# A transformer layer with eight experts: the order of the last pair of tiles, the loading of the first expert matrix, and the order of the last output block

## The chip, the cores and the metric

The kernel runs on one core of a Trainium2 chip. The metric is the device time of one execution in microseconds; lower is better. The core has five engines with queues of their own: TensorE (PE, matrix products; its weight loads are shown as PEld), VectorE (DVE), ScalarE (ACT), GpSimd (POOL) and SyncE (SP), which issues most of the DMAs here. Each engine works through its instructions in the order in which they stand in its queue; semaphores join the queues.

## The reference, cut to what matters

Everything is float32. There are 32 batches of 32 tokens with 512 features (1024 tokens) and a context of 257 rows per batch.

```python
x = x + cross_attention(layernorm(x), ctx)        # one head, 257 keys
x = x + self_attention(layernorm(x))              # 16 heads of 32, rotary, 32 tokens a batch
x = x + experts(layernorm(x))

# experts(xf): 8 experts, the best 2 for each token
scores = sigmoid(xf @ gate_w.T + balance_bias)
top, idx = top_k(scores, 2)
top = top / (top.sum(-1) + 1e-6)
comb[token, idx] = top
h = silu(einsum("td,ehd->teh", xf, w1))           # 512 -> 1024
out = einsum("te,ted->td", comb, einsum("teh,edh->ted", h, w2))
```

## The kernel before, in words

The 1024 tokens are eight tiles of 128 rows, kept in `x_sb`. Two tiles are a pair, `p` from 0 to 3. After the cross-attention comes the self-attention pair by pair, and interleaved with it the routing of the pair before.

The steps of a pair, each a small function in the source:

- `norm`, `turn`: layer norm and transposes through TensorE (tile `yT`).
- `project(p, j, half)`: a quarter of the queries or keys, 16 TensorE instructions (`pp`). A product of 32-bit numbers shows as two instructions.
- `scores(p, i)`: 128 small 32x32 products (`pqs`), then maximum and subtraction on DVE (`smx`, `sex`), exponential on ACT. The PSUM tile has one buffer (`psq`), which `attend` uses too.
- `shares(p, i)`: sum, reciprocal, product and transpose on DVE (`ssm`, `aT`).
- `values(p, tiles)`: the value products (`ppv`) and a copy on ACT.
- `attend(p, i)`: 128 small products (`pos`), then a bias on DVE (`oT`).
- `finish(p, i)`: output projection (`ppo`), addition to `x_sb` on DVE, and a DMA of the row block to the output through SP.
- `norm2(p, i)`: row statistics and the normalized row `fy`, with its token number, for the experts.
- `gate_turn(p, i)`: four transposes of `x_sb` (`fpt`) and a copy on ACT (`fyT`). `gate_logits(p, i)`: eight TensorE instructions with eight columns each (`pg`), then `lg` on DVE. `gate` is both.
- `pick(p)`: the two best experts and their weights, some twenty small DVE instructions with a little ACT and POOL; the running count `cc` is made on POOL, the marks `mk` on DVE.
- `places(p)`: four small products (`pr`) give each token its place in its expert's list, DVE makes it a row number (`pi`), and POOL scatters the rows with four indirect DMAs to the lists `xs_d` in memory.

The loop over `p` = 0, 1, 2 runs the attention of pair `p`, projects pair `p + 1` and routes pair `p - 1`. The last pair (p = 3) is written out behind it. There `order()` ranks the experts by the rows that they have from the first three pairs: four small products (`pn`), seven small DVE instructions, then SP reads the expert numbers into registers and issues the loads: the first expert's `w1` (2 MB in two DMAs), its first 256 rows (`xse`, which must wait until the scatters of the first three pairs have landed), its `w2`, and, after seven more register loads, the second expert's `w1`. `early_turn`, `early_hidden(0)` to `early_hidden(7)` and `early_out` compute these 256 rows of the first expert (`xpe`, `phe`, `poe`) while the last pair is still being routed.

Behind the attention come the remaining rows of the first expert and then the other seven in turn (`turn_rows`, `hidden`, `output`). The list of expert number r in the ranking is computed for `WIDTH[r]` rows: whole blocks of 128 and a part. In `output` a whole block is 16 products of 512 columns (`fpo`), a part is 64 or more small ones (`fpq`); each result is scaled on DVE (`fob`) and added to the output rows by an indirect DMA from POOL that accumulates (`add_rows`, line 194). Rows of a list that hold no token go to spare rows behind the 1024 real ones. Two additions to the output are ordered by a semaphore unless the source declares them independent. The last expert has 160 rows: one block and a part of 32.

The order on each engine is made when the program is built, from the order of the source, by a planner that may put a ready instruction ahead of one that it expects to wait. Buffers of a tile pool are freed by the last reader; the four PSUM buffers `ps` serve most products.

Of the kernel before, what the change touches and what calls it, by code (L numbers as in the profile page):

```python
# [9 lines left out]
F32 = mybir.dt.float32  # L10
# [7 lines left out]
P = 128  # L18
# [4 lines left out]
D = 512  # L23
DC = 384
KD = D // P
# [3 lines left out]
NTT = 8  # L29
NE = 8  # L30
FF = 1024
# [4 lines left out]
WIDTH = (384, 352, 288, 288, 288, 224, 192, 160)  # L36
CAP = max(WIDTH)
NB = CAP // P
EARLY = 2
Q = 32  # L40
YI, YC, YW = D, D + 8, D + 16
# [10 lines left out]
def tile_perceiver_layer(  # L52
# [138 lines left out]
        nc.vector.bn_aggr(mv, st)  # L191

    def add_rows(dst, ob, place, n):
        nc.gpsimd.indirect_dma_start(  # L194
            out=dst,
            out_offset=bass.IndirectOffsetOnAxis(ap=place, axis=0),
            in_=ob,
            in_offset=None,
            bounds_check=n * (NTT * P + P) - 1,
            oob_is_err=True,  # L200
            compute_op=ALU.add,
        )
# [22 lines left out]
    with ExitStack() as attn:  # L225
# [606 lines left out]
        with ExitStack() as sa:  # L832
# [265 lines left out]
            def order():  # L1098

                full = [P, NE, NE]  # L1100
                c = counts(cums[-1], "cnt0")
                key = keep.tile([P, NE], F32, name="key")
                nc.vector.scalar_tensor_tensor(
                    key, c, float(NE), down, op0=ALU.mult, op1=ALU.add
                )
                above = keep.tile(full, F32, name="above")
                nc.vector.tensor_tensor(
                    above,
                    key.unsqueeze(1).to_broadcast(full),
                    key.unsqueeze(2).to_broadcast(full),  # L1110
                    ALU.is_gt,
                )
                rank = keep.tile([P, NE], F32, name="rank")
                nc.vector.tensor_reduce(rank, above, AX.X, ALU.add)

                hot = keep.tile(full, F32, name="hot")
                nc.vector.tensor_tensor(
                    hot,
                    rank.unsqueeze(1).to_broadcast(full),
                    iof.unsqueeze(2).to_broadcast(full),  # L1120
                    ALU.is_equal,
                )
                he = keep.tile(full, F32, name="he")
                nc.vector.tensor_tensor(
                    he, hot, iof.unsqueeze(1).to_broadcast(full), ALU.mult
                )
                eid = keep.tile([P, NE], F32, name="eid")
                nc.vector.tensor_reduce(eid, he, AX.X, ALU.add)
                eidi = keep.tile([P, NE], I32, name="eidi")
                nc.vector.tensor_copy(eidi, eid)  # L1130
                tail["hot"] = hot

                def expert(r):
                    return nc.values_load(
                        eidi[0:1, r : r + 1], engines=[mybir.EngineType.SP],
                        min_val=0, max_val=NE - 1,
                    )


                e = expert(0)  # L1140
                tail["w1"] = {0: expert_w1(e)}
                xs = wk.tile([P, 2, YW], F32, tag="y", name="xse")
                nc.sync.dma_start(
                    xs, xs_d[bass.ds(e * LIST, 2 * P), :].rearrange("(c p) w -> p c w", p=P)
                )
                tail["w2"] = {0: expert_w2(e)}
                tail["e"] = [e] + [expert(r) for r in range(1, NE)]
                tail["w1"][1] = expert_w1(tail["e"][1])
                he0 = keep.tile([P, NE], F32, name="he0")
                nc.vector.tensor_tensor(he0, hot[:, 0, :], c, ALU.mult)  # L1150
                had = keep.tile([P, 1], F32, name="had")
                nc.vector.reduce_sum(had, he0, axis=AX.X)
                mask = keep.tile([P, EARLY], I32, name="mask")
                nc.vector.tensor_scalar(mask, slot[:, 0, 0:EARLY], had, 0.0, ALU.is_lt, ALU.add)
                pl = keep.tile([P, EARLY], I32, name="pl")
                nc.vector.tensor_copy(pl, spare.to_broadcast([P, EARLY]))
                tail["had"] = had
                tail["early"] = {"xs": xs, "mask": mask, "pl": pl}
# [56 lines left out]
            turn(1)  # L1215
            for p in range(NP - 1):
                scores(p, 0)
                project(p + 1, 0, 0)
                shares(p, 0)
                scores(p, 1)  # L1220
                if p:
                    gate(p - 1, 0)
                    gate(p - 1, 1)
                    pick(p - 1)
                project(p + 1, 0, 1)
                shares(p, 1)
                rotate(p + 1, 0)
                attend(p, 0)
                project(p + 1, 1, 0)
                step(norm, p + 2)  # L1230
                attend(p, 1)
                if p:
                    places(p - 1)
                project(p + 1, 1, 1)
                rotate(p + 1, 1)
                finish(p, 0)
                norm2(p, 0)
                finish(p, 1)
                norm2(p, 1)
                if p < NP - 2:  # L1240
                    values(p + 1)
                    step(turn, p + 2)
# [3 lines left out]
            scores(p, 0)  # L1246
            gate_turn(p - 1, 0)
            gate_turn(p - 1, 1)
            scores(p, 1)
            gate_logits(p - 1, 0)  # L1250
            gate_logits(p - 1, 1)
            pick(p - 1)
            values(p, (0,))
            shares(p, 0)
            places(p - 1)
            attend(p, 0)
            values(p, (1,))
            order()
            shares(p, 1)
            finish(p, 0)  # L1260
            norm2(p, 0)
            attend(p, 1)
            gate(p, 0)
            finish(p, 1)
            norm2(p, 1)
            early_turn()
            gate_turn(p, 1)
            early_hidden(0)
            gate_logits(p, 1)
            pick(p)  # L1270
            early_hidden(1)
            early_hidden(2)
            places(p)
            cnt = counts(cums[-1], "cnt")
# [22 lines left out]
    )  # L1297
    idx = keep.tile(full, I32, name="idx")
    nc.gpsimd.iota(
        idx, pattern=[[0, NE], [0, LIST // P]], base=NTT * P, channel_multiplier=1  # L1300
    )
    def parts_of(n):
        return [(c, min(P, n - c * P)) for c in range((n + P - 1) // P)]
# [38 lines left out]
    def short_part(hT, w2, q, place, sh):  # L1342
# [10 lines left out]
                )  # L1353
        ob = fw.tile([P, D], F32, tag="fob", bufs=3, name="fob")
        nc.vector.tensor_scalar_mul(ob[:, 0:w], po[:, 0:w], sh)  # L1355
        add_rows(out.rearrange("r (n w) -> (r n) w", n=n), ob[:, 0:w], place, n)

    def turn_rows(r, xs, n, taken, idx):

# [58 lines left out]
                nc.tensor.transpose(pt[:, k, :], t["hs"][:, ts(h * KD + k, P)], ident)  # L1418
            evac(h, t["hT"][:, h * KD : (h + 1) * KD, 0:P], pt)

    def output(t, w2):

        hT, share, idx = t["hT"], t["share"], t["idx"]
        parts = parts_of(t["n"])
        for c, m in parts:
            if m < P:
                for r0, q in tails_of(m):
                    short_part(
                        hT[:, :, c * P + r0 : c * P + r0 + q], w2, q, *t["spread"].pop(0)
                    )  # L1430
        for c, m in parts:
            if m < P:
                continue
# [5 lines left out]
                )  # L1439
            ob = fw.tile([P, D], F32, tag="fob", bufs=3, name="fob")  # L1440
            nc.vector.tensor_scalar_mul(ob, po, share[:, c : c + 1])  # L1441
            add_rows(out, ob, idx[:, c : c + 1], 1)


    rows_of = {
# [8 lines left out]
    for r in range(1, NE):  # L1454
# [8 lines left out]
        if r == 1:  # L1463
# [1 line left out]
            w1s[2] = expert_w1(eids[2])  # L1465
            rows_of[2] = load_rows(eids[2], 0, WIDTH[2])
            w2s[2] = expert_w2(eids[2])
        output(t, w2s.pop(r))


    over = keep.tile([P, NE + 1], F32, name="over")
# [131 lines left out]
```

## Time and profile before

| | |
|---|---|
| median of 3 runs | 566.55 us (565.16 to 568.67) |
| the profiled execution | 567.44 us |
| its span, first to last instruction | 565.6 us |
| granted TensorE clock, mean | 0.972 |
| PE / DVE / ACT / POOL busy | 93% / 43% / 22% / 19% |
| last pair, from its first scores to `early_out` | 258.6 to 311.6 us |
| remaining rows and other experts | to 554.2 us |

In the profile a line like `L979` is a line of the kernel, `out<-in` names tiles, and `x8` counts instructions. Times are microseconds from the start of the span. Where a line ends with a bracket, it gives the idle time of the engine before it and who ended it. A granted clock of 0.50 means that TensorE got every second pulse.

### The profile page before, as it was taken

To read this page: it belongs to the slowest core of one execution; us is meant where nothing else is said; L and a number is where in the kernel's file an instruction comes from. 1 tells how busy PE (TensorE), PEld (TensorE's weight loads), DVE (VectorE), ACT (ScalarE), POOL (GpSimd) and SP (SyncE) were. 2 spreads that over 40 slices of the span, in tenths; PEclk is the share of its full clock that TensorE was granted. 3 is DMA by queue.
4 is the path that set the end of the run, shared out by engine and by line. 5 is a ranking of instruction groups with operands and counts; after the bars stand their busy time and mean duration, and the time that the engine had idled before them with its cause. 6 is when DMAs were issued, how large, how long until landed. Compare 5 with 4: busy or idle time off the path is not lost.

```text
span 565.6 us, 11308 instructions
## 1 busy us (share of the span) xinstructions
PE 527.2 (93%) x4718; PEld 342.4 (61%) x4718; DVE 243.2 (43%) x706; ACT 123.9 (22%) x274; POOL 105.5 (19%) x185
## 2 busy tenths in 40 slices
PE   6999998999999999998979999999999999999991
PEld 3555554566584875876548456547657475768570
DVE  6564668646667755668534032203122121223120
ACT  3444444322313312212022021002011010102010
POOL 2323445120001012022302110122120202111211
PEclk9899999999999999798989999999999999999997
DMA  7999968999920002012296332647653554756521
GB/s 271 389 376 400 307 248 281 363 393 386 385 84 38 3 21 94 4 41 78 79 366 232 91 92 77 235 135 215 172 167 111 132 192 155 215 159 197 160 27 22
DMA packets 43135, 104.56 MB, mean 185 GB/s; under 512 B 4001, under 2 KB 7233, under 8 KB 42050
## 3 DMA queue, kind: packets, MB, share of 16 engines
q1 hardware_dynamic: 38482, 94.96, 46.9%
q0 software_dynamic: 4592, 8.78, 7.7%
q8 instruction: 39, 0.64, 0.5%
q14 instruction: 22, 0.18, 0.1%
HBM read 75.55 MB, written 28.18 MB: 183 GB/s over the span
## 4 chain that ended last, share of the span: by engine, by line
PE 67%; DMA 2%; DVE 2%; issue 1%; ACT 1%; POOL 0%; POOLq 0%; SPq 0%; ACTq 0%
PE ph L1383 18%; PE fpo L1436 15%; PE pp L387 8%; PE ppv L857 5%; PE fpq L1350 4%; PE phe L1187 3%; PE poe L1201 2%; PE ppo L933 2%; DMA xse<-xs_d 2%; PE pg L979 2%; PE pos L914 2%; PE pqs L872 2%; PE phb L1404 1%; PE xpt L1365 1%; ACT xT L176 1%
## 5 line engine op out<-in xcount | busy, mean ns | idle before, releaser
L1383 PE MATMUL ph<-xT,w 128*128 128x288 f32 (+4 forms) x448 | 100.2, 382 | 3.1 <-ACT xT L176 3.1
L1383 PEld LDWEIGHTS ph<-xT,w 128*128 128x128 f32 x448 | 79.0, 190 | 19.6 <-ACT xT L176 3.7
L1436 PE MATMUL fpo<-w,hT 128*128 128x512 f32 x192 | 84.4, 596 | 0.0
L1436 PEld LDWEIGHTS fpo<-w,hT 128*128 128x128 f32 x192 | 35.9, 190 | 43.9 <-issue 43.7
L1389 DVE TENSOR_TENSOR hT<-ph,sg 128x288 f32<-128x288 f32 (+4 forms) x56 | 23.6, 422 | 62.4 <-ACT sg L1388 62.4
L1441 DVE TENSOR_SCALAR fob<-fpo,share 128x512 f32<-128x512 f32 x12 | 9.0, 751 | 77.0 <-PE fpo L1436 77.0
L1388 ACT ACTIVATE sg<-ph 128x288 f32<-128x288 f32 (+4 forms) x56 | 21.5, 385 | 85.0 <-PE ph L1383 83.4
L194 POOL DMA_INDIRECT out_dram<-fob,idx x12 | 18.6, 1549 | 93.7 <-DVE fob L1441 85.7
L194 POOL DMA_INDIRECT out_dram<-fob,plc x9 | 13.9, 1546 | 101.4 <-DVE fob L1355 85.4
L527 DVE BATCH_NORM_STATS2 st<-n 128x6 f32<-128x384 f32 x64 | 32.5, 545 | 0.0
L176 ACT COPY xT<-xpt 128x512 f32<-128x512 f32 (+2 forms) x12 | 6.0, 497 | 112.5 <-PE xpt L1365 112.4
L933 PE MATMUL ppo<-ao,oT 128*128 128x512 f32 x64 | 30.1, 624 | 0.0
L387 PE MATMUL pp<-syT,aq 128*128 128x256 f32 x96 | 25.6, 427 | 0.0
L482 PE MATMUL pq<-x1T,mq 128*128 128x256 f32 x96 | 24.7, 405 | 0.0
L1071 POOL DMA_INDIRECT xs_d<-fy,pi x16 | 17.0, 1063 | 35.2 <-DVE pi L1067 21.8
L670 PE MATMUL po<-wvo,uT 128*128 128x512 f32 x48 | 22.4, 602 | 1.2 <-ACT uT L663 1.2
L857 PE MATMUL ppv<-av,syT 128*128 128x512 f32 x48 | 23.3, 634 | 0.0
L1350 PE MATMUL fpq<-w,hT 128*32 128x128 f32 (+1 forms) x576 | 22.3, 309 | 0.0
L387 PE MATMUL pp<-syT,ak 128*128 128x256 f32 x96 | 22.3, 385 | 0.0
L387 PEld LDWEIGHTS pp<-syT,aq 128*128 128x128 f32 x96 | 20.2, 215 | 3.3
L933 PEld LDWEIGHTS ppo<-ao,oT 128*128 128x128 f32 x64 | 12.6, 199 | 14.2 <-issue 14.0
L482 PEld LDWEIGHTS pq<-x1T,mq 128*128 128x128 f32 x96 | 18.5, 202 | 4.1 <-issue 1.2
(280 smaller groups left out, 739.7 us busy)
## 6 DMA issues: line engine op xcount, KB each, us to landing
xs_d<-zero SPq DMA_DIRECT2D x8, 2112.0 KB, 20.8
w<-in_w1T_dram SPq DMA_DIRECT2D x16, 1024.0 KB, 8.0
w<-in_w2T_dram SPq DMA_DIRECT2D x16, 1024.0 KB, 7.7
nT<-in_ctxT_dram SPq DMA_DIRECT2D x8, 1542.0 KB, 8.5
n<-in_ctx_dram SPq DMA_DIRECT2D x32, 384.0 KB, 6.3
xs<-xs_d SPq DMA_DIRECT2D x4, 528.0 KB, 7.8
x_sb<-in_x_dram SPq DMA_DIRECT2D x8, 256.0 KB, 7.3
out_dram<-x_sb SPq DMA_DIRECT2D x8, 256.0 KB, 2.0
```

What stands on the lines that cost most here:

```text
L194: nc.gpsimd.indirect_dma_start(out=dst, out_offset=bass.IndirectOffsetOnAxis(ap=place, axis=0), in_=ob, in_offset=None, bounds_check=n * ( ...
L387: nc.tensor.matmul(pp[:, i, :], w[:, k, ts(e, P)], yT[:, k, :], start=(k == 0), stop=(k == KD - 1),)
L482: nc.tensor.matmul(pq[:, 0 : 2 * P], mq[:, k, ts(c, P)], x1T[:, k, :], start=(k == 0), stop=(k == KD - 1),)
L527: nc.vector.bn_stats(st[:, r, :], n[:, r // 2, r % 2, :])
L670: nc.tensor.matmul(po, uT[:, c, :], wvo[:, c, :], start=(c == 0), stop=(c == KC - 1))
L857: nc.tensor.matmul(pp, st[p]["yT"][:, k, ts(i, P)], av[:, k, :], start=(k == 0), stop=(k == KD - 1),)
L933: nc.tensor.matmul(pp, st[p]["oT", i][:, k].rearrange("p b q -> p (b q)"), ao[:, k, :], start=(k == 0), stop=(k == KD - 1),)
L1350: nc.tensor.matmul(po[ts(g, Q), 0:w], hT[:, f, ts(h, Q)], w2[:, f, ts(j, w)], start=(f == 0), stop=(f == KF - 1),)
L1383: nc.tensor.matmul(ph[:, 0:n], w1[:, k, ts(f, P)], t["xT"][:, k, 0:n], start=(k == 0), stop=(k == KD - 1),)
L1388: nc.scalar.activation(sg[:, 0:n], ph[:, 0:n], AF.Sigmoid)
L1389: nc.vector.tensor_mul(hT[:, f, 0:n], ph[:, 0:n], sg[:, 0:n])
L1436: nc.tensor.matmul(po, hT[:, f, ts(c, P)], w2[:, f, :], start=(f == 0), stop=(f == KF - 1),)
```

## The change

Five edits:

1. In the loop, for p = 1 and 2, both `gate_turn` of the pair before stand directly behind the first scores, ahead of a projection; both `gate_logits` stay behind the second scores.
2. In the last pair the third pair's logits and `pick` stand ahead of the second scores, with the first value block between turns and logits; the second value block and `order` stand ahead of the first `attend`. The gate of the last pair's first tile is split in turn and logits, with the second `finish` and `early_turn` between; its second tile's turn comes a hidden product before its logits, and `early_hidden(1)` comes ahead of `pick`.
3. The first expert's `w1` is loaded in halves by columns (512 of 1024) in place of halves by rows, and the 256 rows are asked for between the halves.
4. In the last expert's `output` the whole block stands ahead of the part, and the additions of this call are declared independent of each other.
5. The spare rows get a block of their own for each block of a list, so the output has 1408 rows instead of 1152, of which the first 1024 are used.

```diff
+ROWS = NTT * P + NB * P
     def add_rows(dst, ob, place, n):
-        nc.gpsimd.indirect_dma_start(
+        return nc.gpsimd.indirect_dma_start(
...
-            bounds_check=n * (NTT * P + P) - 1,
+            bounds_check=n * ROWS - 1,
...
                 e = expert(0)
-                tail["w1"] = {0: expert_w1(e)}
+                w1 = ewp.tile([P, KD * FF], F32, tag="ew", name="w1")
+                w1 = w1.rearrange("p (k f) -> p k f", f=FF)
+                tail["w1"] = {0: w1}
                 xs = wk.tile([P, 2, YW], F32, tag="y", name="xse")
-                nc.sync.dma_start(
-                    xs, xs_d[bass.ds(e * LIST, 2 * P), :].rearrange("(c p) w -> p c w", p=P)
-                )
+                for h in range(2):
+                    nc.sync.dma_start(
+                        w1[:, :, ts(h, D)],
+                        w1T[bass.ds(e, 1), :, ts(h, D)].rearrange(
+                            "e (k p) f -> p (e k) f", p=P
+                        ),
+                    )
+                    if h == 0:
+                        nc.sync.dma_start(
+                            xs,
+                            xs_d[bass.ds(e * LIST, 2 * P), :].rearrange(
+                                "(c p) w -> p c w", p=P
+                            ),
+                        )
...
             for p in range(NP - 1):
                 scores(p, 0)
+                if p:
+                    gate_turn(p - 1, 0)
+                    gate_turn(p - 1, 1)
                 project(p + 1, 0, 0)
                 shares(p, 0)
                 scores(p, 1)
                 if p:
-                    gate(p - 1, 0)
-                    gate(p - 1, 1)
+                    gate_logits(p - 1, 0)
+                    gate_logits(p - 1, 1)
                     pick(p - 1)
...
             gate_turn(p - 1, 1)
-            scores(p, 1)
+            values(p, (0,))
             gate_logits(p - 1, 0)
             gate_logits(p - 1, 1)
+            shares(p, 0)
             pick(p - 1)
-            values(p, (0,))
-            shares(p, 0)
+            scores(p, 1)
             places(p - 1)
-            attend(p, 0)
             values(p, (1,))
             order()
+            attend(p, 0)
             shares(p, 1)
             finish(p, 0)
             norm2(p, 0)
             attend(p, 1)
-            gate(p, 0)
+            gate_turn(p, 0)
             finish(p, 1)
             norm2(p, 1)
             early_turn()
+            gate_logits(p, 0)
+            early_hidden(0)
             gate_turn(p, 1)
-            early_hidden(0)
+            early_hidden(1)
             gate_logits(p, 1)
             pick(p)
-            early_hidden(1)
             early_hidden(2)
...
-        idx, pattern=[[0, NE], [0, LIST // P]], base=NTT * P, channel_multiplier=1
+        idx, pattern=[[0, NE], [P, LIST // P]], base=NTT * P, channel_multiplier=1
...
-    def output(t, w2):
+    def output(t, w2, short_first=True):
...
+        adds = []
+        def short():
...
+                        adds.append(
+                            short_part(
+                                hT[:, :, c * P + r0 : c * P + r0 + q],
+                                w2, q, *t["spread"].pop(0),
+                            )
+                        )
+        if short_first:
+            short()
...
-            add_rows(out, ob, idx[:, c : c + 1], 1)
+            adds.append(add_rows(out, ob, idx[:, c : c + 1], 1))
+        if not short_first:
+            short()
+            for i, a in enumerate(adds):
+                for b in adds[:i]:
+                    tc.declare_no_dep(a.ins, b.ins, reason="rows of their own")
...
-        output(t, w2s.pop(r))
+        output(t, w2s.pop(r), r + 1 < NE)
```

More of the change, by code (lines that the diff above doesn't have):

```diff
@@ L1355, in short_part @@
         nc.vector.tensor_scalar_mul(ob[:, 0:w], po[:, 0:w], sh)
-        add_rows(out.rearrange("r (n w) -> (r n) w", n=n), ob[:, 0:w], place, n)
+        return add_rows(out.rearrange("r (n w) -> (r n) w", n=n), ob[:, 0:w], place, n)
     def turn_rows(r, xs, n, taken, idx):
@@ L1419, in turn_hidden @@
             evac(h, t["hT"][:, h * KD : (h + 1) * KD, 0:P], pt)
-    def output(t, w2):
+    def output(t, w2, short_first=True):
         hT, share, idx = t["hT"], t["share"], t["idx"]
         parts = parts_of(t["n"])
[L1425 to L1430, printed above, removed]
+        adds = []
+        def short():
+            for c, m in parts:
+                if m < P:
+                    for r0, q in tails_of(m):
+                        adds.append(
[6 more added lines that the diff above has]
+            short()
         for c, m in parts:
@@ L1596 @@
     args["out"] = nc.dram_tensor(
-        "out_0_dram", (NTT * P + P, D), F32, kind="ExternalOutput"
+        "out_0_dram", (ROWS, D), F32, kind="ExternalOutput"
     ).ap()
```

## The prediction

> **What bounds the kernel now.** I read the page first (busy times, granted clock), then TensorE's waits and its timeline where the change works, then the clock by stretch, then the chain that ended last.
>
> ```profile
> PE 527.2 (93%) x4718; PEld 342.4 (61%) x4718; DVE 243.2 (43%) x706; ACT 123.9 (22%) x274; POOL 105.5 (19%) x185
> PEclk9899999999999999798989999999999999999997
> ```
> TensorE (PE) is busy 93% of the span, so only its idle time and its slow time can be won. The clock row has dents at slices 14, 16, 18 and 20 (198 to 297 us): the second half of the self-attention, which the change rearranges.
>
> ```profile
> PE pg L979 <- ACT fyT L972: 3.0, 2, 2.3
> PE pg L979 <- DVE sex L882: 2.0, 1, 2.0
> PE phe L1187 <- issue: 1.7, 1, 1.7
> ```
> These are PE's waits from 225 to 330 us (engine, line <- releaser: us, times, longest). The logits `pg` wait three times, for the copy of their turned tile, or in line with it.
>
> ```profile
> 259.85 1.10 PE L970 MATMUL fpt<-ident,x_sb 128*128 128x128 f32 x8
> 262.99 0.39 PE L979 MATMUL pg<-gwc,fyT 128*128 128x8 f32 x2 [2.04 <-DVE sex L882]
> 263.31 1.41 PE L872 MATMUL pqs<-sqk,sqk 32*32 32x32 f32 x128
> 264.65 3.15 PE L979 MATMUL pg<-gwc,fyT 128*128 128x8 f32 x14
> ```
> This is the head of the last pair. The first logits stand ahead of the second scores here although the source has them behind: the program's order fills gaps, so source order is a guide, not a promise. The 14 `pg` took 0.22 us each; the eight at 192.22 took 1.06, 0.13 each. The difference is the clock:
>
> ```profile
> 195.80:199.20 3.40, 3.40 (x10) 2.70 (x9) 3.18 (x18) 0.20 (x1) 0.40 (x2) 0.50 0.00 0
> 233.40:240.20 6.80, 6.80 (x85) 5.76 (x85) 4.43 (x23) 0.79 (x2) 0.40 (x2) 0.50 0.01 2
> 264.10:270.90 6.80, 6.80 (x76) 4.98 (x63) 5.91 (x24) 0.84 (x2) 0.59 (x1) 0.50 0.01 2
> 288.00:291.40 3.40, 3.40 (x6) 1.32 (x5) 0.11 (x1) 0.00 (x0) 0.00 (x0) 0.50 1.03 398
> 334.80:554.20 219.40, 216.27 (x1315) 141.99 (x1312) 48.78 (x160) 27.99 (x69) 30.95 (x20) 1.00 0.52 156
> ```
> Stretch: its length, busy times, and third from the end the granted clock. Four stretches, 20.4 us together, ran at half clock: about 10 us lost, more than all the waits. Each follows a mix of 32x32 products, transposes and 8-column logits. Behind 334.8 PE is 98.6% busy at full clock, so what is won before arrives at the end undiminished.
>
> ```profile
> 547.10 7.08 PE fpo L1436 x16
> 554.18 0.03 issue
> 554.20 0.76 DVE fob L1441
> 554.96 0.03 issue
> 555.00 0.50 POOLq L1486
> 555.50 1.28 POOL out_dram L194
> ```
> The end of the chain: the last full block, its scaling, its addition to the output. That addition lands 5.1 us after its start (555.23), at 560.3; closing semaphores take the span to 565.6.
>
> **What the Trainium skill says.** TensorE: Matmul & The Clock Gate, Part 1: the clock is halved after an idle window of about 3.4 us, restored after a busy one, and the windows run freely. The trace agrees in the lengths (3.4 and 6.8 us at 0.50) but not in "idle": PE shows 100% busy inside them, and before 233.4 it was idle only 0.73 us. Short products evidently count for little. DMA: Bandwidth & Descriptors, Anatomy of one DMA: about 2.0 us fixed plus bytes over 436 GB/s, most of the fixed part being the receipt of the write. The two last additions landed after 3.3 us (64 KB) and 5.1 us (256 KB), a larger difference than that slope gives; I use the measured ones. The same page, Rules for kernel authors: an accumulating DMA must wait for an earlier access of the same bytes. That is the wait the change drops between two additions, and the wider spare rows keep their rows apart.
>
> **The change, part by part**, against the profiled execution's 567.44 us (span 565.6 plus 1.8).
>
> *Loop, second and third passes.* The turns of the gates move ahead of a dense projection, logits follow the second scores. Instructions are the same; the ACT copy now has 3.7 us of projection to hide in. Removed: PE's waits of 0.67 (at 192.22) and 0.73 us (at 232.40): **-1.4**. The half clock cost (3.4 + 6.8)/2 = 5.1 us here, e.g. the projection of 16 took 5.35 us instead of 3.72. Eight turns leave the thin stretch, but 16 logits still stand together, 16 x 0.13 = 2.1 us beside 1.2 us of scores: a 3.4 us window that covers them can still count as idle. Bounds: none of the three windows saved (0), all (-5.1). I take one: **-1.7**. DVE, ACT and POOL receive their work later by the projection at most; the places of these passes have 10 us of slack on POOL.
>
> *Last pair.* From 258.64 to 311.55 us is 52.9 us. PE at full clock, start to start: scores 2.4, turns 2.2, logits 3.7, values 7.0, places and counts 1.6, attention 2.4, output projections 7.0 (6.96 per 16, at 251.68), expert turn 1.0, hidden 64 x 0.218 = 13.95. Sum 41.3. The rest, 11.6, is waits (2.04 + 2.27 + 0.24 + 1.71 = 6.3) and half clock (10.2/2 = 5.1).
> Afterwards: (a) the first value block (3.5 us) stands between turns and logits, and the copies end at 263.42: the 2.04 goes. (b) Attention loses its cover: the value block that stood behind it goes ahead, so the first output projection waits for oT on DVE, possibly behind the seven small operations of the order (278.53 to 280.38, 1.85): 1.85 - 1.21 + 0.69, so 0 to 1.4, I take 1.2. (c) Second attention to second projection was 3.78 us from 283.24 to 287.02 with turn and logits inside; oT ended at 285.34, 2.1 us after attention, behind the row statistics. With only the turn inside: 1.5 idle, instead of 2.27. (d) From the end of the projection (292.40) to the first hidden product was 3.47 us, set by DVE's turned copy (295.09, behind the statistics). Expert turn and logits fill 1.9 to 2.1 of it: 1.4 idle. (e) Places wait for choice and counter; the second value block can fill: 0.3, up to 1.5. Sum 4.4 instead of 6.3: **-1.9** (0 to -3.5). Clock: three windows now; 2.1 us of logits still stand together and (c) stays thin, so I take two: **-1.7** (0 to -5.1).
> The scatters, moved with the choice, start some 4 us sooner on POOL, which is empty there (idle 5.1 us before 276.23).
>
> *First matrix in halves.* Same 2 MB, and rows of 2 KB instead of 4 KB; the second matrix already has such rows and its two halves landed 2.7 us apart (295.3, 298.0) like the first's. The rows of the expert pass in front of one half: 1 MB less ahead of them. They landed at 292.6, and PE waited 0.24 for them. Order and scatters are sooner as well, so I expect them at 284 to 286, before they are asked for at some 286. The half behind them is needed from the fifth hidden product on, 9 us later. On SP the rows' wait for the scatters now holds back the second half and the second matrix; cover: the latter is first needed at 311.6, 13 us after it landed. Cost **0**; without that cover up to 2.7, the time of one half.
>
> *Last block ahead of part.* The 16 products of the block start at 545.2 instead of 547.1, end at 552.3; scaled at 553.05; addition starts 553.35, lands 5.1 later: 558.4. The part's 64 products (1.88) end at 554.2, scaling 0.35 (at 547.17), POOL is free at 554.9 plus the 0.3 between DMAs: start 555.2, landing 3.3 later: 558.5, up to 559.2 if the two share the queue. Against 560.36: **-1.5** (-1.2 to -1.9). Without the dropped dependency the second would wait for 558.4 and this would become a loss of 1.4. The numbers of the spare rows and a wider output cost no instruction.
>
> Sum: -1.4 - 1.7 - 1.9 - 1.7 - 1.5 = **-8.2**: 567.4 becomes 559.2. The median of three runs is 0.9 lower than the profiled one (566.55), so **558.3** is my prediction.
>
> **Rivals.** *Clock kept, 0.22*: the thin stretches stay thin, all six windows remain, and only waits and end are won: 1.4 + 1.5 + 0 to 1.9, so 561.5 to 564. For it: 16 logits in a row; against it: turns taken out. The same figure results if the planner's gap filling restores the old order in the last pair. *Clock freed, 0.16*: four or more windows go: 8.2 + 2 x 1.7 or more, 551 to 555. *DVE decides the last pair, slower, 0.12*: after the second scores DVE has 1.4 (scores) + 2.4 (order and mask) + 0.7 (places) + 0.7 (oT) + 2.3 (shares) = 7.5 us, besides 2.9 of the choice, before the first output projection's input is certain; PE has values, counts and attention, 5.2 us, to hide it. If DVE's order puts oT last and places wait in line, PE idles 5 us there, the second attention as much again, and each idle stretch brings a half-clock window (1.7): 13 lost against 8.2 won, 571. It decides once the wait in front of the first `ppo` passes 6 us. Against it: DVE ran these same operations in 14 us before and PE never waited for oT.
> The forecast, 555 to 561: 0.50.
>
> **How the numbers follow.** Range 552 to 565: it takes in the forecast, most of both faster rivals, and leaves out slower runs and the far end of the freed clock. About 1% (5.7 us) is what a measurement here can tell from none. Faster by over 1% (below 560.9): 0.48 + 0.16 + 0.02 = 0.66. Within: 0.24. Slower: 0.10.
>
> **What would show it.** Right: no wait of `pg` in loop and head of the last pair; rows of the first expert landed before the expert turn; last addition of 128 columns landing about 1.5 us earlier behind PE's end; half clock under 15 us in all. Wrong: a wait of `ppo` on oT over 3 us, `xpe` waiting for its rows, `pr` waiting on DVE or POOL, or half clock again 20 us.

## The result, and the profile after

The changed kernel takes 557.02 us (median of 4 runs, 555.81 to 559.04) against 566.12 us (median of 4, 565.16 to 568.67) for the kernel before: a ratio of 0.985, 95% interval 0.9818 to 0.9881, which is 9.1 us less. The profiled execution took 559.04 us, with a span of 557.3 us and a mean granted clock of 0.985.

In the profiled executions the 8.4 us that the span lost lie as follows (each stage from the start of the first instruction named to that of the next one, from the timelines):

| stage | before | after | difference |
|---|---|---|---|
| second loop pass to the last pair (first `pqs` of each) | 73.8 | 67.0 | -6.8 |
| last pair, to the first `poe` | 52.9 | 52.2 | -0.7 |
| remaining rows and other experts, to PE's end | 242.6 | 242.4 | -0.2 |
| PE's end to the end of the span | 11.5 | 10.7 | -0.8 |

So in these two profiles the loop gave nearly all, and the last pair, which the change rearranges most, almost nothing. The page of the changed kernel, busy times and granted clock in 40 slices:

```profile
PE 520.1 (93%) x4718; PEld 337.6 (61%) x4718; DVE 241.9 (43%) x706; ACT 123.2 (22%) x274; POOL 106.1 (19%) x185
PEclk9899999999999999999799999999999999999997
```

PE does the same 4718 instructions in 7.1 us less of busy time: that is clock, not work. Counted from 0, the clock row of before has dents at slices 16, 18 and 20 (at 14 it shows a 9, though the prediction names that slice too). In the changed kernel one is left between 180 and 300 us, at slice 19. PE's waits from 180 to 330 us in the changed kernel (engine, line, what for: us in total, times, longest us):

```profile
PE pos L915 <- issue: 3.2, 7, 0.5
PE ppo L934 <- DVE oT L922: 2.3, 2, 1.6
...
PE phe L1202 <- issue: 0.5, 1, 0.5
PE pr L1050 <- DVE sg L1026: 0.4, 1, 0.4
```

No logits `pg` wait any more, in the loop or in the head of the last pair. Two waits of the output projection on `oT` have come (0.8 and 1.6), as forecast, and one that nobody had in the sum: `pos`, the 128 small products of the first attention, seven times, with no releaser. The timeline of PE at that place, changed kernel (start, length, instructions; in the bracket the idle time before):

```profile
265.44 0.57 PE L915 MATMUL pos<-aT,v 32*32 32x32 f32 x42
266.31 0.27 PE L915 MATMUL pos<-aT,v 32*32 32x32 f32 x4 [0.30 <-issue]
267.06 0.27 PE L915 MATMUL pos<-aT,v 32*32 32x32 f32 x4 [0.49 <-issue]
...
270.75 0.88 PE L915 MATMUL pos<-aT,v 32*32 32x32 f32 x63 [0.52 <-issue]
272.42 6.21 PE L934 MATMUL ppo<-ao,oT 128*128 128x512 f32 x8 [0.79 <-DVE oT L922]
278.57 1.29 PE L915 MATMUL pos<-aT,v 32*32 32x32 f32 x128
```

The second attention has its 128 products done in 1.29 us. The first takes 6.2: after 42 products PE goes on in steps of one to six with half a microsecond between, and nothing that the profile records releases them. And `ppo` behind it takes 6.21 us in place of 3.70. The clock by stretch says why (length, busy times of PE, PEld, DVE, ACT, POOL, then granted clock, DMA share, GB/s; changed kernel):

```profile
190.00:235.00 45.00, 44.69 (x835) 32.84 (x837) 30.35 (x83) 10.53 (x23) 7.91 (x14) 1.00 0.10 38
264.00:270.70 6.70, 3.53 (x72) 2.08 (x70) 3.23 (x10) 0.71 (x2) 3.98 (x4) 1.00 0.36 141
270.70:277.50 6.80, 5.96 (x69) 2.94 (x70) 1.47 (x8) 0.00 (x0) 0.00 (x0) 0.50 0.37 115
327.00:546.60 219.60, 216.47 (x1315) 142.10 (x1313) 49.14 (x160) 27.94 (x69) 30.24 (x20) 1.00 0.51 155
```

The loop now runs at full clock. During the stall PE is busy 3.53 of 6.70 us, and the 6.8 us behind it run at half clock: two windows, 3.4 us lost. So 4.9 us of stall (6.2 less 1.29) and 3.4 us of clock stand against what the last pair won in this profile. The last row is the large remainder, unchanged.

The end, first by the chain that ended last, then by the timeline, both of the changed kernel:

```profile
539.97 4.72 PE fpo L1464 x11
544.69 2.54 PE fpq L1369 x64
547.23 0.03 issue
547.26 0.36 DVE fob L1374
547.62 0.03 issue
547.65 0.99 POOLq L1520
548.64 0.79 POOL out_dram L195
```

```profile
545.76 1.54 POOL L195 DMA_INDIRECT out_dram<-fob,idx  x1 [15.98 <-DVE fob L1469]
547.26 0.35 DVE L1374 TENSOR_SCALAR fob<-fpq,shq 128x128 f32<-128x128 f32 x1 [1.77 <-PE fpq L1369]
547.88 1.55 POOL L195 DMA_INDIRECT out_dram<-fob,plc  x1 [0.58 <-DVE fob L1374]
```

The part `fpq` now comes last, and its addition starts 0.6 us after POOL is through with that of the block (545.76 + 1.54 = 547.30). PE ends at 546.58, but the small scaling starts 0.68 us later, at 547.26, just as POOL ends its work on the block's addition.

### The profile page after: what moved, and what is told of

Read it like the earlier page. It is cut to its first block, busy times and chain, and to the rows that moved or that the text cites. A ratio compares the mean times of both kernels' runs of the same rounds, so it can differ in the third digit from the quotient of the medians.

```text
span 557.3 us, 11309 instructions
## 1 busy us (share of the span) xinstructions
PE 520.1 (93%) x4718; PEld 337.6 (61%) x4718; DVE 241.9 (43%) x706; ACT 123.2 (22%) x274; POOL 106.1 (19%) x185
## 4 chain that ended last, share of the span: by engine, by line
PE 68%; DVE 3%; issue 2%; ACT 1%; POOL 0%; POOLq 0%; ACTq 0%
PE ph L1402 18%; PE fpo L1464 15%; PE pp L388 8%; PE ppv L858 4%; PE ppo L934 4%; PE fpq L1369 4%; PE phe L1202 3%; PE poe L1216 3%; PE pos L915 2%; PE pqs L873 1%; PE phb L1423 1%; PE xpt L1384 1%; PE pg L980 1%; ACT xT L177 1%; PE po L671 1%
## 5 line engine op out<-in xcount | busy, mean ns | idle before, releaser
L388 PE MATMUL pp<-syT,aq 128*128 128x256 f32 x96 | 22.1, 383 | 0.0
L858 PE MATMUL ppv<-av,syT 128*128 128x512 f32 x48 | 21.3, 594 | 0.0
L1369 PEld LDWEIGHTS fpq<-w,hT 128*32 128x32 f32 x576 | 16.2, 110 | 7.1 <-issue 3.2
```

The source lines that it names most:

```text
L388: nc.tensor.matmul(pp[:, i, :], w[:, k, ts(e, P)], yT[:, k, :], start=(k == 0), stop=(k == KD - 1),)
L858: nc.tensor.matmul(pp, st[p]["yT"][:, k, ts(i, P)], av[:, k, :], start=(k == 0), stop=(k == KD - 1),)
L1369: nc.tensor.matmul(po[ts(g, Q), 0:w], hT[:, f, ts(h, Q)], w2[:, f, ts(j, w)], start=(f == 0), stop=(f == KF - 1),)
```

## The experiments

The theory was the prediction's: half clock and waits make up the gain, edit by edit. The rivals: the single edits don't add up, because they share the same half-clock windows (stretches of about 3.4 us at a granted clock of 0.50); the stall of `pos` is a matter of instruction fetch, of the scatters from POOL beside it, or of the edit that it came with. The intervals are those of the ratio to the kernel before, run on the same chip.

**The edits one by one.** Edit 1 in the kernel before:

```diff
                 scores(p, 0)
+                if p:
+                    gate_turn(p - 1, 0)
+                    gate_turn(p - 1, 1)
                 project(p + 1, 0, 0)
...
-                    gate(p - 1, 0)
-                    gate(p - 1, 1)
+                    gate_logits(p - 1, 0)
+                    gate_logits(p - 1, 1)
```

> The kernel before with the first edit alone (turns a product ahead of logits in the second and third pass). Theory of the prediction: the waits of 0.67 and 0.73 us go and one of three half-clock windows, -3.1 us. Theory from the two traces: the thin stretch was what halved the clock, so all three windows of these passes go with the waits: -6 to -6.5 us (560), and the last pair still takes 52.9 us from its first scores to the first expert's output. Rival (the loop gained only because the windows happened to fall well in the one profiled execution): between -1.4 and -3, with windows at half clock still seen between 190 and 245 us.

Measured: 560.27 us against 565.25, ratio 0.9906 (0.9874 to 0.9937), so about -5.3 us (-3.6 to -7.1). The stretches that stood at half clock before, in this kernel:

```profile
190.00:199.00 9.00, 9.00 (x294) 7.79 (x294) 6.53 (x24) 2.40 (x6) 0.86 (x2) 1.00 0.02 4
228.00:245.00 17.00, 17.00 (x453) 14.89 (x454) 12.64 (x39) 3.38 (x9) 1.85 (x3) 1.00 0.02 4
```

PE is without a gap and at full clock in both. All three windows of this stage are gone, not one, and with them both waits.

How many windows the old order has is a matter of the single execution, though. In the four profiles with the old loop (before, edit 2 alone, edit 3 alone, edits 4 and 5 alone) the stage from the second pass to the last pair has 10.2, 3.4, 6.8 and 3.4 us at half clock. In the ten with edit 1 it has none, but for 3.4 us in one. The stage takes 70.9 to 73.8 us in the four and 66.5 to 68.3 us in the ten: 5.0 us less in the mean, which agrees with the 5.3.

Edit 2 in the kernel before:

```diff
-            scores(p, 1)
+            values(p, (0,))
             gate_logits(p - 1, 0)
             gate_logits(p - 1, 1)
+            shares(p, 0)
             pick(p - 1)
-            values(p, (0,))
-            shares(p, 0)
+            scores(p, 1)
             places(p - 1)
-            attend(p, 0)
             values(p, (1,))
             order()
+            attend(p, 0)
...
-            gate(p, 0)
+            gate_turn(p, 0)
...
             early_turn()
+            gate_logits(p, 0)
+            early_hidden(0)
             gate_turn(p, 1)
-            early_hidden(0)
+            early_hidden(1)
             gate_logits(p, 1)
             pick(p)
-            early_hidden(1)
...
```

> The kernel before with the second edit alone (order of the last pair). Theory of the prediction: -3.6 us. Theory from the two traces: the waits and windows won are given back by a stall of TensorE inside the first attention, 128 small products in 6.2 us instead of 1.3, and by the half clock that follows it: -0.5 to -2 us, and the stall is seen again at the same instruction. Rival (the stall is an accident of one execution): -7 to -9 us, no stall.

Measured: 556.18 us, ratio 0.982 (0.9794 to 0.9846): -10.2 us (-8.7 to -11.6), from this edit alone. PE's waits in this kernel from 180 to 330 us, and the clock of its last pair:

```profile
PE ppo L933 <- DVE oT L921: 2.4, 2, 1.6
PE xpe L1169 <- DMA xse<-xs_d: 1.6, 1, 1.6
PE pg L979 <- ACT fyT L972: 1.4, 2, 0.7
...
PE pr L1049 <- DVE sg L1025: 0.4, 1, 0.4
```

```profile
245.50:297.00 51.50, 46.92 (x688) 32.20 (x687) 31.86 (x121) 12.52 (x23) 13.95 (x22) 1.00 0.54 202
```

The last pair is 46.6 us long in place of 52.9, at full clock throughout, and `pos` hardly stalls (1.83 us for 128 products). The two `pg` waits are those of the loop, which this kernel keeps. The rows of the first expert are late by 1.64 us: asked for behind 2 MB.

Edits 4 and 5 alone (block ahead of part with the independent additions, and the wider spare rows), and edit 3 alone (the halves of `w1` by columns, the rows between them):

```diff
...
-        output(t, w2s.pop(r))
+        output(t, w2s.pop(r), r + 1 < NE)
```

> The kernel before with the last block ahead of the part, the additions independent and the wider spare rows. Theory of the prediction: -1.5 us (-1.2 to -1.9). Theory from the two traces: the scaling of the part on VectorE waits some 0.7 us behind the descriptors of the block's addition on GpSimd, so -0.7 to -1.0 us, and the scaling starts 0.6 us or more after the part's last product.

```diff
+                for h in range(2):
+                    nc.sync.dma_start(
+                        w1[:, :, ts(h, D)],
...
+                    if h == 0:
+                        nc.sync.dma_start(
+                            xs,
...
```

> The kernel before with the third edit alone (first matrix in halves by columns, the 256 rows between). All theories: the rows land 1 to 2.7 us sooner than 9.5 us after their issue; the expert turn stands behind the second output projection and waited only 0.24 us for them, so 0 to -0.3 us. If the rows had been the bound of this stage: -1 us or more.

Measured: 565.02 us, ratio 0.998 (0.9958 to 1.0002), for the tail, so -1.1 us with 0 at the edge of the interval; 564.77 us, ratio 0.9991 (0.9969 to 1.0014), for the halves, no difference. In the profile of the tail alone the part's addition starts 1.03 us after PE's end, as forecast, but it takes 5.3 us to land in place of 3.3, and from PE's end to the end of the span it is 11.7 us, against 11.5 before.

The four add up to some -17 us, against -9.1 for all together. Part of that is the measure: in the profile of edit 2 alone the loop stage, which it doesn't touch, is 2.9 us shorter than before. Half-clock windows fall differently from one execution to the next: 39 executions of the kernel before on this chip took 562 to 570 us, and those with a mean clock of 0.981 took 562.0 to 563.6, with 0.975 564.7 to 566.2, with 0.969 567.9 to 569.8. A single profile is one draw of the windows.

**Both orders together.** Edits 1 and 2 in the kernel before:

```diff
+                    gate_turn(p - 1, 0)
+                    gate_turn(p - 1, 1)
...
+            values(p, (0,))
...
+            scores(p, 1)
...
```

> The kernel before with the first two edits alone. If loop and last pair add up: -5 and -9, about 551. If the stall is a matter of these two together: 557 to 558, with the stall in the profile, and the halves of the matrix and the tail are worth 0 to 1 us.

Measured: 555.52 us against 565.87, ratio 0.9834 (0.9782 to 0.9885). PE's wait on the rows and the half-clock stretch of this kernel:

```profile
PE xpe L1169 <- DMA xse<-xs_d: 1.2, 1, 1.2
```

```profile
258.60:265.40 6.80, 6.56 (x11) 3.38 (x12) 4.80 (x19) 0.63 (x1) 2.43 (x4) 0.50 0.10 41
```

No stall, the loop at 66.7 us, the last pair at 49.2: with both orders two windows of half clock are back in the last pair, in front of the attention. So even without a stall the gains of the two edits don't add up: 15.5 singly (on one chip) against 9.4 (6.5 to 12.3) together (on another).

The change without edit 3:

```diff
-                for h in range(2):
-                    nc.sync.dma_start(
-                        w1[:, :, ts(h, D)],
...
+                tail["w1"] = {0: expert_w1(e)}
...
```

> The changed kernel without the third edit: the first matrix in halves by rows, the 256 rows behind both. Theory of the prediction: 0 (the rows come in time either way). From the run with the last pair alone, where TensorE waited 1.6 us for these rows: with the stall, which holds TensorE back while the rows travel, 0 to 1; without it 1.5 to 2.7 us more than the changed kernel.

Measured: 556.73 us, ratio 0.9839 (0.9798 to 0.9881), the same as the whole change, which was not run on this chip. There is no stall, the rows are late by 1.36 us, and the last pair takes 46.4 us at full clock; but one window of half clock fell into the loop and two in front of it.

**The stall.** First the changed kernel once more, without an edit, on the chip of the next three runs (moved stream, attention first, dropped dependency):

> The changed kernel once more, unchanged. If the stall of the first attention of the last pair (128 products in 6.2 us in place of 1.3, in steps of about 0.66 us) is part of how this kernel runs: about -9 us against the kernel before, and the profile shows it again at the same product. If it is an accident of one execution: no stall in this profile and a time near what the single edits add up to, -14 us (551).

Measured: 556.96 us against 566.42, ratio 0.9837 (0.9816 to 0.9857). The stall is there again, shorter: `pos` from 266.28 to 269.17. The scatters of the third pair lie at 262.55 to 267.45 here, 264.99 to 269.89 in the first profile.

The stream of PE moved by 32 small products at the start of the program, which change no output:

```diff
...
+    for i in range(32):
+        nc.tensor.matmul(
+            pn_[:, 8 * i : 8 * i + 8], ones, ident[:, 0:8], start=True, stop=True
+        )
```

> The changed kernel with 32 small products (64 matrix instructions and 64 weight loads) added at the start, where TensorE has nothing to do; they move every later instruction of TensorE by 128 places in its stream, and compute nothing that is used. Theory that the stall comes from the fetching of TensorE's instructions, at the border of a block[...] that falls inside the 128 products: the stall moves or goes, and the time falls by 5 to 8 us against the changed kernel (549 to 552). Rival, that the scatters of GpSimd which run at the same moment slow these products: stall and time stay (557).

Measured: 570.79 us, ratio 1.0081 (1.006 to 1.0103). The added products were not free, as the expectation took them to be: PE is at them for 13.8 us, from 1.68 us on, and its next product starts at 15.43, against 2.31 in the changed kernel beside it. The first scores come 12 us later, so the time says nothing; the last pair is as long as in the changed kernel (52.5 us). Its first attention:

```profile
277.47 0.90 PE L921 MATMUL pos<-aT,v 32*32 32x32 f32 x42
278.88 0.28 PE L921 MATMUL pos<-aT,v 32*32 32x32 f32 x4 [0.51 <-issue]
...
281.10 0.94 PE L921 MATMUL pos<-aT,v 32*32 32x32 f32 x77 [0.53 <-issue]
```

It stalls at the same product, the 43rd, with the stream of instructions moved. So a border at a fixed place of the stream is not the cause, unless the fetched blocks are so short that the shift is a whole number of them. Nor did PE wait for a packet of instructions that was on its way: between 278.4 and 281.1 neither of the two instruction queues moved one. What the five profiles with a stall share is the count from the start of the attention: PE halts first after 42 to 45 of its products, though the scatters began between 0.45 and 3.7 us before it. A limit in how PE is supplied with instructions is thus not ruled out as a part of the cause.

The first attention ahead of the places and the order:

```diff
-            places(p - 1)
             values(p, (1,))
-            order()
             attend(p, 0)
+            places(p - 1)
+            order()
```

> The changed kernel with the second value block and the first attention of the last pair ahead of places and order, so that the third pair's scatters run beside the output projection and not beside the 128 small products. Rival theory (scatters slow the small products): no stall, 5 to 8 us less than the changed kernel. Theory of instruction fetch: the border of the block lies in the same attention, eight instructions earlier in the stream than before, so the stall can stay, and the time with it (556 to 558). Either way the order of the experts comes 1.5 us later, and TensorE may wait for the 256 rows by 0 to 1.5 us.

Measured: 558.42 us, ratio 0.986 (0.9835 to 0.9884). PE's attentions in it, and the first and last of POOL's scatters:

```profile
262.28 1.29 PE L915 MATMUL pos<-aT,v 32*32 32x32 f32 x128
269.02 0.86 PE L915 MATMUL pos<-aT,v 32*32 32x32 f32 x45
270.38 0.27 PE L915 MATMUL pos<-aT,v 32*32 32x32 f32 x5 [0.51 <-issue]
...
272.58 0.85 PE L915 MATMUL pos<-aT,v 32*32 32x32 f32 x74 [0.52 <-issue]
```

```profile
266.87 1.06 POOL L1072 DMA_INDIRECT xs_d<-fy,pi  x1 [7.26 <-DVE he L1165]
...
270.78 0.98 POOL L1072 DMA_INDIRECT xs_d<-fy,pi  x1 [0.30 <-issue]
```

The first attention, now in front of the scatters, is free; the second, beside them, stalls, until 0.82 us after the last of them. The stall goes with the scatters. In all five profiles that have one it ends 0.74 to 0.86 us after POOL's work on the last scatter. It goes with that work rather than with the scattered data: here no packet of the scatters, and none of instructions, started between 269.9 and 272.5 us. The rows are late by 2.8 us here.

The changed kernel with the scatters of the third pair put off on POOL by two additions, PE's stream the same:

```diff
...
+                    for _ in range(2):
+                        nc.gpsimd.tensor_tensor(late, late, zero, ALU.add)
...
```

> The changed kernel with about 3 us of additions on GpSimd ahead of the third pair's scatters; TensorE's stream is the same, instruction for instruction. Theory that the scatters cause the stall: the first attention of the last pair runs its 128 products in 1.3 us, and a stall appears, if at all, in the second attention, ended within 1 us of the end of the last scatter. Theory that TensorE's own stream causes it (a border of a fetched block): the stall stays in the first attention. Time: the 256 rows come some 3 us later, so a gain of up to 8 us from the missing stall and its half clock may be given back in part: 551 to 557.

Measured: 557.28 us against 565.87, ratio 0.9835 (0.9783 to 0.9887). Both attentions end in 1.29 us; the scatters lie between them, 268.34 to 273.23. That agrees with the scatters as the cause, but proves little alone: on this chip three kernels with such an overlap did not stall either (below). And the time is that of the change: PE waits for the rows in place of the stall, and 10.2 us of the last pair are at half clock. PE's waits:

```profile
PE xpe L1191 <- DMA xse<-xs_d: 3.4, 1, 3.4
PE ppo L934 <- DVE oT L922: 2.6, 2, 1.6
```

The first attention between the places and the second value block:

```diff
             places(p - 1)
+            attend(p, 0)
             values(p, (1,))
             order()
-            attend(p, 0)
```

> The changed kernel with the first attention of the last pair put between places and the second value block; TensorE then has it behind three quarters of that block, ahead of most of the scatters. If the scatters are the cause and only products issued more than half a microsecond into them suffer: no stall or a short one, 3 to 8 us less than the changed kernel (549 to 554). If a stall meets the second attention instead: no gain.

Measured: 552.71 us (551.73 to 555.93), ratio 0.9797 (0.9751 to 0.9843), the lowest of all. PE in its last pair:

```profile
263.07 1.82 PE L915 MATMUL pos<-aT,v 32*32 32x32 f32 x128
264.83 1.13 PE L858 MATMUL ppv<-av,syT 128*128 128x512 f32 x2
...
266.15 3.68 PE L934 MATMUL ppo<-ao,oT 128*128 128x512 f32 x8
...
277.20 1.09 PE L1184 MATMUL xpe<-ident,xse 128*128 128x128 f32 x8 [0.31 <-DMA xse<-xs_d]
```

The last quarter of the value block (PE had already run six of its eight products) covers the copy of `oT`, so the first `ppo` doesn't wait; no stall, though POOL's scatters (263.84 to 268.73) overlap this attention; rows late by 0.31; full clock; last pair 45.4 us. It ran on one chip with the three kernels with both orders, without edit 3 and with later scatters, and its median is 2.8, 4.0 and 4.6 us below theirs, with overlapping intervals; the unedited change was not run beside it, so by how much it beats that is not settled.

So a stall was seen only beside the scatters, and the other attention of the same profiles, away from them, took 1.29 us; but the scatters don't suffice. In four kernels (edit 2 alone, edits 1 and 2, the change without edit 3, the attention between) `pos` overlapped them and took only 1.6 to 1.8 us, with one or two halts of under 0.3 us. With edit 2 alone and without edit 3 the first scatter starts 0.45 us before `pos`, just as in the first profile of the change, and PE's products around it stand in the same order. Four of the five profiles with a stall come from one chip (which chip the first profile of the changed kernel ran on isn't recorded), these four kernels from two others. This points to the chip more than to the program. But no run shows the unedited change on one of the other two chips, so the cause stays open.

The last pair takes 52.8 to 54.3 us in the four profiles without edit 2 and 52.2 to 53.6 us in the five with a stall, but 45.4 to 49.2 us in the four kernels just named. In the whole times this doesn't show as clearly (0.9839 without edit 3 and without a stall, 0.9837 for the change with it); these two come from different chips, and windows of half clock in other stages add to them.

**The dropped dependency.** The change without it:

```diff
-            for i, a in enumerate(adds):
-                for b in adds[:i]:
-                    tc.declare_no_dep(a.ins, b.ins, reason="rows of their own")
```

> The changed kernel with the dependency between the last two additions kept. The part's addition then waits for the landing of the block's, 5.1 us after its start, before its own 3.3 us: 2.5 to 3.5 us more than the changed kernel. Rival (the additions overlap little anyway): 0 to 1 us more.

Measured: 561.22 us, ratio 0.9907 (0.9885 to 0.993), 4.3 us more than the changed kernel beside it. Its last two additions:

```profile
545.35 1.54 POOL L195 DMA_INDIRECT out_dram<-fob,idx  x1 [15.98 <-DVE fob L1469]
546.86 0.35 DVE L1374 TENSOR_SCALAR fob<-fpq,shq 128x128 f32<-128x128 f32 x1 [1.78 <-PE fpq L1369]
550.84 1.55 POOL L195 DMA_INDIRECT out_dram<-fob,plc  x1 [3.94 <-DMA out_dram<-fob,idx]
```

POOL stands 3.94 us for the landing of the block's addition; from PE's end to the end of the span it takes 13.2 us, against 10.5 and 10.7 in the two profiles of the change. That is 2.6 to 2.8 of the 4.3. The rest agrees with the stall, which took 4.4 us in this profile and 2.9 in that of the change beside it.

## Why the prediction was right, point by point

- **The time** was 558.3 and the measurement 557.0. That the sum is so close is luck, for its errors cancel: in the two profiles the loop gave 6.8 us for the 3.1 forecast, the last pair 0.7 for 3.6, the end 0.8 for 1.5. The clock's share in the loop was set too low, the last addition's landing too short, and a stall was not foreseen.
- **Loop, waits (-1.4):** right, both are gone.
- **Loop, clock (-1.7, one of three windows):** a mis-sized term. In the pair of profiles all three went, 5.1 us, and with the waits that makes 6.5 of the 6.8. But the profile of before, from which three were counted, had more of them than the other three with the old loop (3.4 to 6.8 us at half clock). The mean of the four, 6.0 us, is worth 3.0 us, so the loop's gain is nearer to 4.4 with the waits; alone it measured 5.3 (3.6 to 7.1). The reason given for the caution, 16 logits that still stand together, didn't hold: nine of ten profiles with edit 1 have no window there. Whether the moved turns or the closed gap did it isn't separated.
- **Last pair, waits (-1.9, 4.4 left):** the size was right, the parts weren't. With edit 2 alone 4.5 us are left: 0.8 for (b), forecast at 1.2; 1.56 for (c), at 1.5; 0.1 for (d), at 1.4; 0.4 for (e), at 0.3; and 1.64 for the rows, at 0. In the changed kernel 3.2 are left besides the stall, with the rows in time. That DVE puts the order in front of `oT` didn't come about.
- **Last pair, clock (-1.7, one of three windows):** all three went with edit 2 alone. In the changed kernel's profile two are there, behind the stall; with both orders and no stall two as well, in front of the attention. Over the ten profiles with edit 2 the last pair has from none to 13.7 us at half clock, 6.8 in the mean, which is the two windows that the prediction left standing. Before there were 10.2, and 10.2 to 17.1 in the other three with the old order. So the value was fair for the mean, and the number of windows in one execution can't be told from the order alone.
- **The stall (4.9 us, 1.6 in the second profile of the same kernel):** in no step and no rival. The prediction wrote that the scatters start sooner "on POOL, which is empty there" and gave that move no price on PE. That was the step that failed: it asked what POOL had to do, and not what ran beside the scatters. It is also why the last pair's forecast of -3.6 isn't met where the stall appears (last pair 52.2 to 53.6 us) and is met or passed in the four overlapping kernels without it (45.4 to 49.2).
- **Halves (0):** right for itself (ratio 0.9991). The rows themselves do come sooner: 6.4 us from asking to landing with the halves (edit 3 alone, the attention between), against 9.5 before and 8.2 with edit 2 alone. In the changed kernel they were asked for at 274.8, in place of 283.1, and DVE used them at 281.9, before the forecast 284 to 286. So the edit may well be worth something in the new order, where PE comes earlier: without it the rows are late by 1.2 to 1.6 us in the three kernels that have edit 2 and the old loading, with it by 0.3 with the attention between. Whether the total gains from it isn't shown (0.9839 without, 0.9837 with it, on different chips).
- **Tail (-1.5):** the measured -1.1 (-2.4 to +0.1) doesn't tell it from 0. The two profiles differ by 0.8. What was mis-sized is the landing: 3.3 us was read from a part's addition that ran alone, but behind the block's addition it took 5.3 (tail alone), 5.1 (without edit 3, and with the attention between) and 3.6 us (scatters later). The prediction's "up to 559.2 if the two share the queue" left 0.7 us for that. The late start of the scaling in the changed kernel costs less than its 0.68 us: the addition starts 1.30 us after PE's end, against 1.03 where the scaling starts at once and the addition waits for POOL's work on the block's. The dependency matters: without its removal the tail is 2.6 to 2.8 us longer; the forecast of "a loss of 1.4" instead of a gain of 1.5 is a difference of 2.9.
- **Rivals:** DVE did not decide (waits for `oT` 0.8 and 1.6, far from the 6 us). "Clock kept" falls. "Clock freed", 551 to 555, is what the version with the attention between shows (552.7), and not the change.
- **Signs:** of those named for right, three came: no wait of `pg`, the rows in time, and 10.2 us of half clock before PE's end. The 1.5 us at the end did not. Of those named for wrong only a wait of `pr` on DVE came, and at 0.4 us it had little weight.
- **The Trainium skill** (TensorE: Matmul & The Clock Gate, Part 1) has windows of about 3.4 us that run freely. Every half-clock stretch before PE's end, in all profiles of this case, has 3.4 or 6.8 us but one, of 10.2, with edit 3 alone. Its word "idle" is about the window ahead of the half clock, and the prediction's figure of 100% busy inside it doesn't speak to that. Behind the stall it fits: PE was busy 3.53 of the 6.70 us ahead. With both orders it doesn't: PE was busy 3.20 of the 3.40 us ahead of 258.60, with logits and scores; nor does it in the kernel before, with 0.73 us of idleness ahead of 233.4. The 39 executions agree with windows that fall by chance: a step of 0.006 in the mean clock, two windows of 3.4 us in 566, goes with some 3 us.

## What to carry to other kernels

Where a stretch of short products lies in front of dense ones, look at the granted clock behind it: each window of 3.4 us at half clock costs up to 1.7 us (half its length, an estimate), and in the profile of before they cost more than all the waits together. Dense work put between the short products removed them from the loop in nine of ten profiles, from the last pair not reliably. Count the windows in several profiles, not in one. Test edits of one stage singly and together: -17 in parts became -9, and the lowest time, though by a margin that is not settled, came from neither, but from the change with one step moved so that a copy hides behind the rest of a block. And when a step moves, ask what will run beside each of its DMAs, not only whether its queue is free.

## What was not expected of the hardware

- Bursts of 32x32 products on PE went in steps of one to six, some 0.5 us apart, while POOL issued indirect DMAs, and were free 0.74 to 0.86 us after the last; 2.9 to 6.2 us for work of 1.29. The first 42 to 45 products always passed. Five profiles show it, at least four of them from one chip; in four other kernels, with such an overlap on other chips, it cost 0.3 to 0.6 us. The cause is open.
- A DVE scaling from PSUM by a column started 0.68 us after its product ended, and in five profiles within 0.06 us of the end of POOL's work on an indirect DMA; in four others it started 0.06 to 0.07 us after the product, with POOL still at work. The Trainium skill (SBUF — State Buffer, Who interferes with whom) says that a DVE instruction with at most one SBUF input, outside its two-port modes, does not contend with GpSimd. These five profiles look like a case where it does; no run isolates it. They are the same five as those with the stall, and the code up to this scaling is the same in all nine, which again points to the chip.
- The 64 instructions of 32 products with eight columns, at the very start of the program, took 13.8 us, 0.22 us each. The logits of eight columns took 0.22 us each at half clock and 0.13 us each at full clock.
